# Two preactivation blocks in one kernel: the background work's big transfers counted double, and one operand load asked for earlier

## The chip, the cores and the metric

The kernel runs on one core of a Trainium2 chip. The metric is the device time in microseconds (us) of one execution. Five engines work side by side, each through its own instruction list in order: PE (TensorE, matrix products), DVE (VectorE), ACT (ScalarE), POOL (GpSimd) and SP (SyncE). Here SP does nothing but issue DMA transfers; every transfer of this kernel is issued from SP, so a transfer that has to wait for its data or its buffer holds back all that stand behind it in SP's list.

## The reference

The input `x` is 16 images of 64 x 64 pixels and 96 channels. Two blocks follow each other, each with a residual: `x = x + block(groupnorm(x))`.

```
# block 0: a two-layer channel MLP with a quadratic activation, on an image upsampled by
# two and band-limited (done here with small dense matrices); low-passed, every 2nd pixel kept
h = upsample(xn);  h = h @ W1.T + b1
h = coef0 + coef1 * h + coef2 * h * h
h = h @ W2.T + b2;  out = lowpass(h)[::2, ::2]

# block 1: a selective-scan block. d = 192 inner channels, 16 states, 4 scan directions
xz = x @ in_proj.T;  xc, z = split(xz);  z = silu(z)
xc = silu(depthwise_conv3x3(xc) + conv_b)
xs = [xc rows, xc columns, xc rows reversed, xc columns reversed]        # K = 4 directions, L = 4096
dts, Bs, Cs = split(x_proj @ xs);  delta = softplus(dt_proj @ dts + bias)
h_t = exp(delta_t * A) * h_(t-1) + (delta_t * u_t) * B_t                 # for every channel and state
y_t = sum over the states of h_t * C_t,  plus u_t * D
y = y0 + y2[::-1] + transposed(y1 + y3[::-1])
y = layernorm(y) * w + b;  out = out_proj @ (y * z)
```

The recurrence in `h_t` is the bulk of the work: 16 images x 4 directions x 192 channels x 16 states, each a chain of 4096 steps.

## The kernel before

**The foreground.** The function `scan` runs over 3072 *units*. A unit is one image, one quarter of the 4096 positions (`T` = 1024), one of six *blocks* (two groups, e = 1 and e = 0, of 32 channels in one direction) and one `j` (four of the 16 states). A block has four units, j = 0 to 3; a *step* (one pair of directions, one quarter) has six blocks, 24 units; an image has eight steps, 192 units. In the text "unit 101" is the unit counted from the start of its image.

In unit n the work on the engines is:

- POOL, `drive(n + 2)` (L794): b = dtu x B for both groups of the unit after next (128 x 2048).
- ACT, `decay(n + 1, e)` (L788), once for each group: da = exp(A x delta), into one PSUM tile for each group.
- DVE, `recur(n, e)` (L803 or L805), once for each group: the recurrence itself, a scan over 1024 positions.
- The product with C: for group 0 on DVE (L972), for group 1 on POOL (L963). In one unit of five (`SHARE`), called odd here, group 1's product is done on DVE as well (L954).
- PE, `read_out(n - 1)` (L827): sums over the states.

The order of a unit is written out by hand (the schedule is manual): group 1's scan, `decay(n + 1, 1)`, **slot 0**, POOL's product and `drive(n + 2)`, group 0's scan, `read_out(n - 1)`, **slot 1**, group 0's product, `decay(n + 1, 0)`, the store of a finished block, **slot 2**, and then loads for later units.

**The loads of the foreground.** For the block after the present one, `dtu` is asked for in the unit with j = 0, the tile `delta` of group 1 in the unit with j = 1, and the tile `delta` of group 0 in the unit with j = 2, behind slot 2. `delta` tiles have three buffers, so group 0's tile of the next block takes the place of group 1's tile of the present block. The last reader of that one is `decay(n + 1, 1)` of the unit with j = 2, which stands just ahead of slot 0. All these are issued at L715, 512 KB each. The B and C rows (`bt`, `ct`, L734) are asked for behind slot 2 too.

**The background.** Between the scans two other programs are advanced bit by bit: `front(mi + 1)`, which does block 0 and the convolution of the next image, and after it `finish(mi - 1)`, which does the layernorm and the output product of the image before. Both are Python generators: what lies between two `yield`s is a *slice*. A third generator, `project`, makes dtu, delta, B and C for the next step of 24 units. Each of the three slots of a unit calls `slot(position)`, which first takes a slice of `project` where one is due and then one of `front` or `finish`. A slice of these is due while `n * POS < at * SLICES`, where `at` counts the slots so far (`POS` = 576 an image), and `n` the slices taken: one for each, or the number that the generator yielded, so `HEAVY` counts as two. One slice at most is taken in a slot.

`front` begins with `parts(xt, xc[mi])`, the load of the next image in four transfers of 384 KB, one a slice. Then comes `norm` (two passes over the image on ACT, a few tiny operations, and at L237 `nb = nmean * rg` on DVE, 96 x 1), a small DVE addition `lin` (L260, 96 x 96), the four sweeps of block 0, the output of block 0 stored by `parts(made["x1"], x1)`, `norm` again, and twelve convolution tiles. After the matrix products of each tile the generator yields `WAIT`: the two Silu activations (L506, L507) need another ACT table set, so they run only in a slot 2 with no store pending (the gate). The unit after a gate is made odd, and while the gate is fresh `project` is held where it has yielded `BUSY`. At the end `parts(made["xs"][1], col)` stores 2 MB in four transfers. `finish` begins with two more `parts`, six loads of 512 KB (`ycol`, issued at L200 as all of `parts`).

Of the kernel before, what the change touches and what calls it, by code (L numbers as in the profile page):

```python
# [68 lines left out]
NEPS = 1e-5  # L69
BOTH = "natural_log_exp_and_others"  # L70
POS = 3 * 8 * 6 * NQ
SLICES = 499
WAIT = -1
BUSY = -2
HEAVY = 2
# [5 lines left out]
def tile_two_blocks(  # L81
# [114 lines left out]
    def parts(out, in_, n=4):  # L196

        step = L // n
        for i in range(n):
            nc.sync.dma_start(out=out[:, step * i:step * i + step], in_=in_[:, step * i:step * i + step])  # L200
            yield

    def norm(xt):

# [418 lines left out]
    def scan():  # L623


        with ExitStack() as es:
# [85 lines left out]
            def spread(out, what, ctx, bi, e):  # L712

                v, s0, r = blocks[bi]
                nc.sync.dma_start(  # L715
                    out=out,
                    in_=ctx[what][v][32 * (s0 + e):32 * (s0 + e) + 32, :].unsqueeze(1).to_broadcast([32, NQ, T]),
                )

            def fetch_dtu(ctx, bi):  # L720
                t = p2.tile([128, 2, T], F32, name="dtu")
                for e in range(2):
                    spread(t[:, e, :], "dtu", ctx, bi, e)
                return t

            def fetch_delta(ctx, bi, e):
                t = p3.tile([128, T], F32, name="delta")
                spread(t, "delta", ctx, bi, e)
                return t
# [11 lines left out]
            def fetch_y0(lc, bi):  # L741
                y0 = yp.tile([128, 2 * QT], F32, name="y0")
                nc.sync.dma_start(out=y0, in_=ypart[lc, bi])
                return y0
# [6 lines left out]
            bc, dtus, deltas = {}, {}, {}  # L751
# [33 lines left out]
            def decay(n, e):  # L785
                k, g = group(n, e)
                da = aps.tile([128, T], F32, name="da", tag=f"da{e}")
                nc.scalar.activation(da, deltas[n // NQ, e], AF.Exp, scale=a_s[:, k, g, units[n][2]:units[n][2] + 1])  # L788
                das[n, e] = da

            def drive(n):
                b = p4.tile([128, 2, T], F32, name="b")
                bt = bc[0, blocks[units[n][1]][2], units[n][2]]
                nc.gpsimd.tensor_mul(b, dtus[n // NQ], bt.unsqueeze(1).to_broadcast([128, 2, T]))  # L794
                bs[n] = b

            def recur(n, e, out):
                st, bi, j = units[n]
                pair = steps[st][1]
                da, b = das.pop((n, e)), bs[n][:, e, :]  # L800
                before = 0.0 if st % NT == 0 else states[bi][0][:, e, j:j + 1]
                if pair == 0:
                    nc.vector.tensor_tensor_scan(out, da, b, before, ALU.mult, ALU.add)  # L803
                else:
                    nc.vector.tensor_tensor_scan(out[:, ::-1], da[:, ::-1], b[:, ::-1], before, ALU.mult, ALU.add)  # L805

            def keep(n, e, h, copy):
                st, bi, j = units[n]
                if st % NT < NT - 1:
                    end = h[:, T - 1:T] if steps[st][1] == 0 else h[:, 0:1]  # L810
                    copy(states[bi][1][:, e, j:j + 1], end)  # L811
# [70 lines left out]
            def slot(position):  # L882
                nonlocal full, full_unit
                back = ahead_gen if ahead_gen.gen is not None else behind_gen
                back.at += 1
                step_gen.at += 1
                gate = back.said == WAIT and back.due() and position == 2 and storing is None
                if gate:
                    full, full_unit = 2, n + 1
                if step_gen.due() and not (full and step_gen.said == BUSY):  # L890
                    light = step_gen.said != BUSY
                    step_gen.step()

                    if light and step_gen.due() and step_gen.said != BUSY:
                        step_gen.step()
                if back.due() and (gate or back.said != WAIT):
                    back.step()
                full = max(full - 1, 0)

            last = len(units) - 1  # L900
            def next_step(st, mi):

                nonlocal step_gen
                if st < len(steps):
                    if steps[st][0] > mi:
                        ahead_gen.drain()
                    step_gen = Background(project(*steps[st], ctxs[st], gps), PSLICES, 3 * per_step)
# [8 lines left out]
            for n, (st, bi, j) in enumerate(units):  # L916
                mi, pair, lc = steps[st]
                v, s0, r = blocks[bi]
                m = n // NQ
                if n % per_image == 0:  # L920
                    image[mi]["y"] = dram.tile([2, DI, L], F32, name="y_d")
                    behind_gen.drain()
                    ahead_gen = behind_gen = nothing
                    if mi + 1 < B:
                        ahead_gen = Background(front(mi + 1), SLICES, POS)
                elif n % per_image == 2 and mi > 0:
                    behind_gen = Background(finish(mi - 1), SLICES, POS)
                if j == 0:
                    new = stp.tile([128, 2, NQ], F32, name="new", tag=f"st{bi}")
                    states[bi] = (states[bi][1] if states[bi] else None, new)  # L930

                if j == 0:
                    ahead = None
                    if bi + 1 < len(blocks):
                        ahead = ctxs[st], bi + 1
                    elif n + NQ <= last:
                        step_gen.drain()
                        ahead = ctxs[st + 1], 0
                        next_step(st + 2, mi)
                    if ahead:  # L940
                        dtus[m + 1] = fetch_dtu(*ahead)
                elif j == 1:
                    if ahead:
                        deltas[m + 1, 1] = fetch_delta(*ahead, 1)


                credit += 1
                odd_here = n == full_unit or credit >= SHARE
                if odd_here:
                    credit -= SHARE  # L950
                h = das[n, 1] if odd_here else bs[n][:, 1, :]
                recur(n, 1, h)
                if odd_here:
                    nc.vector.tensor_mul(bs[n][:, 1, :], h, bc[1, r, j])  # L954
                keep(n, 1, h, nc.scalar.copy if odd_here else nc.vector.tensor_copy)
                if n < last:
                    decay(n + 1, 1)
                slot(0)
                if storing is not None:
                    next(storing, 0)  # L960
                    storing = None
                if not odd_here:
                    nc.gpsimd.tensor_mul(h, h, bc[1, r, j])  # L963
                if n + 2 <= last:
                    drive(n + 2)

                h = das[n, 0]
                recur(n, 0, h)
                if n >= 1:
                    read_out(n - 1)  # L970
                slot(1)
                nc.vector.tensor_mul(bs[n][:, 0, :], h, bc[1, r, j])  # L972
                keep(n, 0, h, nc.scalar.copy)
                if n < last:
                    decay(n + 1, 0)
                if n >= 1 and units[n - 1][2] == NQ - 1:
                    storing = store(n - 1)
                    next(storing)
                slot(2)
                if j == 2 and ahead:  # L980
                    deltas[m + 1, 0] = fetch_delta(*ahead, 0)
                if j == NQ - 1 and n < last and steps[units[n + 1][0]][1] == 1:
                    st2, bi2, _ = units[n + 1]
                    y0s[steps[st2][2], bi2] = fetch_y0(steps[st2][2], bi2)


                at = n % per_step
                for what in range(2):
                    ahead_j = at - (2 * NQ - 1 + what)
                    if 0 <= ahead_j < NQ:  # L990
                        bc[what, 1, ahead_j] = fetch_bc(ctxs[st], 1, ahead_j, what)
                    ahead_j = at - (5 * NQ - 1 + what)
                    if 0 <= ahead_j < NQ and st + 1 < len(steps):
                        bc[what, 0, ahead_j] = fetch_bc(ctxs[st + 1], 0, ahead_j, what)
# [113 lines left out]
```

## Time and profile before

| what | value |
|---|---|
| time, median of 3 runs | 21079.41 us (21074.11 to 21098.74) |
| the profiled execution, own time | 21085.42 us |
| its span, first to last instruction | 21083.6 us |
| DVE busy | 19569.4 us, 93% of the span |
| POOL busy | 19498.8 us, 92% |
| PE busy | 16908.7 us, 80% |
| ACT busy | 13780.9 us, 65% |
| first scan starts, last scan ends | 494 us, 20917 us |

The profile counts an engine as busy from an instruction's start to its end, also where the instruction itself is held up inside. The first 494 us (the first image's `front`, before any scan) and the last 166 us (the last image's `finish`) lie outside the scans. DVE and POOL are nearly always busy in between; so the table alone doesn't tell which of them sets the time in which stretch. That is read from the waits of each, and from the order in time.

### The profile page before, as it was taken

What the parts mean: (1) busy time and instruction counts of PE and PEld (TensorE: products, weight loads), DVE (VectorE), ACT (ScalarE), POOL (GpSimd) and SP (SyncE); (2) the same over time, 40 slices, a digit from 0 to 9 for tenths busy, and PEclk for the clock granted to TensorE, in tenths of its full rate; (3) what the DMA queues carried; (4) which work ended last, traced back from release to release, by engine and by line L of the source; (5) the groups of instructions that cost most, each with busy time, mean ns of one, the idle gap of its engine ahead of it and who ended that gap; (6) DMA issues with size and microseconds to landing.
All of it is one profiled execution on the core that took longest, in us unless ns stands there. A gap on an engine that the chain in (4) does not pass through costs nothing. (4 is left out here: it accounts for less than half of the span.)

```text
span 21083.6 us, 273452 instructions
## 1 busy us (share of the span) xinstructions
PE 16908.7 (80%) x98988; PEld 7230.6 (34%) x98988; DVE 19569.4 (93%) x12983; ACT 13780.9 (65%) x20546; POOL 19498.8 (92%) x5538
## 2 busy tenths in 40 slices
PE   7876788888878788788788888888787787888856
PEld 4423324233343333324333242333433333243221
DVE  0999999999999999999999999999999999999997
ACT  4666666667666666666666666676666666666553
POOL 0999999999999999999999999999999999999996
PEclk8887888888889888898888988888898888988977
DMA  2565565655656566565665656556565665656654
GB/s 84 191 202 195 195 227 195 221 202 196 226 198 227 197 210 212 194 230 191 218 207 197 226 199 219 202 197 222 197 226 198 212 212 198 229 195 216 224 186 141
DMA packets 1855464, 4277.11 MB, mean 203 GB/s; under 512 B 449438, under 2 KB 548670, under 8 KB 1852062
## 3 DMA queue, kind: packets, MB, share of 16 engines
q1 hardware_dynamic: 1854110, 4259.62, 60.1%
q8 instruction: 781, 12.80, 0.3%
q14 instruction: 573, 4.69, 0.1%
HBM read 3380.58 MB, written 878.18 MB: 202 GB/s over the span
## 5 line engine op out<-in xcount | busy, mean ns | idle before, releaser
L794 POOL TENSOR_TENSOR b<-dtu,bt 128x2048 f32<-128x2048 f32 x3072 | 13895.8, 4532 | 581.2 <-DMA dtu<-dtu_d 465.1
L788 ACT ACTIVATE da<-delta,a_s 128x1024 f32<-128x1024 f32 x6144 | 6857.4, 1117 | 2562.1 <-DVE b L972 945.5
L963 POOL TENSOR_TENSOR b<-b,ct 128x1024 f32<-128x1024 f32 x2458 | 5797.1, 2358 | 836.9 <-DVE new L811 628.6
L827 PE MATMUL y<-b,fold_s 128*32 128x256 f32 x49152 | 3871.3, 437 | 1153.0 <-DVE b L972 680.8
L972 DVE TENSOR_TENSOR b<-da,ct 128x1024 f32<-128x1024 f32 x3072 | 3756.4, 1223 | 91.8
L803 DVE TENSOR_TENSOR_SCAN da<-da,new,b 128x1024 f32<-128x1024 f32 x1383 | 3245.3, 2347 | 72.7 <-ACT da L788 57.2
L805 DVE TENSOR_TENSOR_SCAN da<-da,new,b 128x1024 f32<-128x1024 f32 x1361 | 3193.0, 2346 | 99.7 <-ACT da L788 77.0
L827 PEld LDWEIGHTS y<-b,fold_s 128*32 128x32 f32 x49152 | 1388.5, 119 | 3876.9 <-issue 1464.0
L805 DVE TENSOR_TENSOR_SCAN b<-da,new,b 128x1024 f32<-128x1024 f32 x943 | 2208.7, 2342 | 139.3 <-ACT da L788 81.5
L803 DVE TENSOR_TENSOR_SCAN b<-da,new,b 128x1024 f32<-128x1024 f32 x921 | 2156.5, 2341 | 11.2 <-ACT da L788 10.5
L811 ACT COPY new<-da 128x1 f32<-128x1 f32 x2764 | 432.9, 157 | 2607.4 <-DVE b L972 2236.0
L488 PE MATMUL c_ps<-xgp,wtap_s 96*64 96x512 f32 (+1 forms) x4608 | 1728.2, 633 | 184.7 <-ACT row L506 179.4
L697 PE MATMUL s<-w,ident_s 128*128 128x512 f32 x1530 | 1167.2, 854 | 636.0 <-ACT w L692 614.2
L371 PE MATMUL h_ps<-xu,w1t_s 96*128 96x500 f32 x1920 | 1044.0, 643 | 299.9 <-ACT t L311 125.9
L383 PE MATMUL o_ps<-w2c_s,hsq 128*100 128x96 f32 x9600 | 1041.5, 266 | 178.1 <-ACT hsq L352 177.8
L677 PE MATMUL s<-pr,dtw_s 128*128 128x512 f32 x1530 | 928.5, 691 | 315.2 <-ACT delta L703 224.9
L805 DVE TENSOR_TENSOR_SCAN da<-da,b 128x1024 f32<-128x1024 f32 x482 | 1103.5, 2289 | 53.0 <-ACT da L788 43.1
L383 PEld LDWEIGHTS o_ps<-w2c_s,hsq 128*100 128x100 f32 x9600 | 975.0, 179 | 410.3 <-ACT hsq L352 232.1
L803 DVE TENSOR_TENSOR_SCAN da<-da,b 128x1024 f32<-128x1024 f32 x460 | 1053.0, 2289 | 36.8 <-ACT da L788 34.8
L697 PE MATMUL s<-e,ident_s 128*128 128x512 f32 x1530 | 1004.2, 745 | 0.0
L820 PE MATMUL y<-y,ident_s 128*128 128x512 f32 x768 | 524.2, 770 | 583.5 <-ACT yt L838 457.6
L488 PEld LDWEIGHTS c_ps<-xgp,wtap_s 96*64 96x64 f32 (+1 forms) x4608 | 583.1, 169 | 1121.7 <-issue 842.6
(143 smaller groups left out, 21936.5 us busy)
## 6 DMA issues: line engine op xcount, KB each, us to landing
dtu<-dtu_d SPq DMA_DIRECT2D x1536, 512.0 KB
delta<-delta_d SPq DMA_DIRECT2D x1536, 512.0 KB
bt<-rows SPq DMA_DIRECT2D x1024, 512.0 KB
ct<-rows SPq DMA_DIRECT2D x1024, 512.0 KB
u<-xs_d SPq DMA_DIRECT2D x893, 256.0 KB
dtu_d<-dtu SPq DMA_DIRECT2D x765, 256.0 KB
delta_d<-delta SPq DMA_DIRECT2D x765, 256.0 KB
xr<-in_x SPq DMA_DIRECT2D x768, 128.0 KB
```

What stands on the lines that cost most here:

```text
L371: nc.tensor.matmul(h_ps[j], lhsT=w1t_s[:, 128 * j:128 * (j + 1)], rhs=xu.rearrange("c p q -> c (p q)"), start=True, stop=True,)
L383: nc.tensor.matmul(o_ps[:, p, :], lhsT=hsq[j][:, UPS * p:UPS * (p + 1)], rhs=w2c_s[:, j, :], start=(j == 0), stop=(j == HB - 1),)
L488: nc.tensor.matmul(c_ps[p:p + n], lhsT=wtap_s[:, tap, 128 * i:128 * i + n], rhs=xgp[:, h0:h0 + 8, dx:dx + HW], start=(tap == 0), stop=(tap ...
L677: nc.tensor.matmul(s, lhsT=dtw_s[:, pair, v, :], rhs=pr, start=True, stop=True)
L697: nc.tensor.matmul(s, lhsT=ident_s, rhs=of, start=(k == 0), stop=(k == 3))
L788: nc.scalar.activation(da, deltas[n // NQ, e], AF.Exp, scale=a_s[:, k, g, units[n][2]:units[n][2] + 1])
L794: nc.gpsimd.tensor_mul(b, dtus[n // NQ], bt.unsqueeze(1).to_broadcast([128, 2, T]))
L803: nc.vector.tensor_tensor_scan(out, da, b, before, ALU.mult, ALU.add)
L805: nc.vector.tensor_tensor_scan(out[:, ::-1], da[:, ::-1], b[:, ::-1], before, ALU.mult, ALU.add)
L827: nc.tensor.matmul(y[32 * q:32 * q + 32, e, :], lhsT=fold_s, rhs=b[:, e, QT * q:QT * q + QT], start=(pair == 0 and j == 0 and e == 0), sto ...
L963: nc.gpsimd.tensor_mul(h, h, bc[1, r, j])
L972: nc.vector.tensor_mul(bs[n][:, 0, :], h, bc[1, r, j])
```

## The change

There are three edits. `parts` yields `HEAVY` in place of nothing, so that each of its slices counts as two. `SLICES` goes from 499 to 517: an image has 12 `parts` slices in `front` and 6 in `finish`, and 499 + 18 = 517, so that the background ends at the same place. The load of group 0's `delta` for the next block moves from behind slot 2 to directly behind slot 0 of the same unit.

```
-SLICES = 499
+SLICES = 517
...
         for i in range(n):
             nc.sync.dma_start(out=out[:, step * i:step * i + step], in_=in_[:, step * i:step * i + step])
-            yield
+            yield HEAVY
...
                 if n < last:
                     decay(n + 1, 1)
                 slot(0)
+                if j == 2 and ahead:
+                    deltas[m + 1, 0] = fetch_delta(*ahead, 0)
                 if storing is not None:
                     next(storing, 0)
                     storing = None
...
                 slot(2)
-                if j == 2 and ahead:
-                    deltas[m + 1, 0] = fetch_delta(*ahead, 0)
                 if j == NQ - 1 and n < last and steps[units[n + 1][0]][1] == 1:
```

No instruction is added or removed on any engine; what changes is where the background's instructions stand among the scans, and where one load of each block stands in SP's list.

More of the change, by code (lines that the diff above doesn't have):

```diff
@@ L71 @@
 POS = 3 * 8 * 6 * NQ
-SLICES = 499
+SLICES = 517
 WAIT = -1
@@ L200, in parts @@
             nc.sync.dma_start(out=out[:, step * i:step * i + step], in_=in_[:, step * i:step * i + step])
-            yield
+            yield HEAVY
     def norm(xt):
@@ L958, in scan @@
                 slot(0)
+                if j == 2 and ahead:
+                    deltas[m + 1, 0] = fetch_delta(*ahead, 0)
                 if storing is not None:
@@ L979, in scan @@
                 slot(2)
-                if j == 2 and ahead:
-                    deltas[m + 1, 0] = fetch_delta(*ahead, 0)
                 if j == NQ - 1 and n < last and steps[units[n + 1][0]][1] == 1:
```

## The prediction

> **What bounds the kernel now.** I read the page's busy shares first, then the waits of POOL and DVE, then the order in time at the places where POOL waits.
>
> ```profile
> PE 16908.7 (80%) x98988; PEld 7230.6 (34%) x98988; DVE 19569.4 (93%) x12983; ACT 13780.9 (65%) x20546; POOL 19498.8 (92%) x5538
> L794 POOL TENSOR_TENSOR b<-dtu,bt 128x2048 f32<-128x2048 f32 x3072 | 13895.8, 4532 | 581.2 <-DMA dtu<-dtu_d 465.1
> L963 POOL TENSOR_TENSOR b<-b,ct 128x1024 f32<-128x1024 f32 x2458 | 5797.1, 2358 | 836.9 <-DVE new L811 628.6
> ```
>
> POOL's two rows make up its whole busy time: 4.53 us in each unit and 2.36 in four of five, 6.42 us a unit. DVE needs two scans of 2.34, a product of 1.23, a second one in one unit of five, and some small things: 6.4 us too. The scans last from 494 to 20917 us, 6.65 us a unit. So POOL and DVE bound it together. POOL works 19494 us of these 20423 and idles 930, some 60 us an image in images 1 to 14, and to that idle time I reduce the change: a DVE stall under which POOL still has work costs nothing by itself.
>
> POOL's waits by releaser:
>
> ```profile
> POOL b L963 <- DVE new L811: 628.6, 296, 14.1
> POOL b L963 <- issue: 131.1, 53, 6.2
> POOL b L794 <- PE y L827: 87.6, 30, 3.8
> ```
>
> It waits for DVE's scans, hardly ever for a transfer. Summed by unit, the 60 us an image lie in three places: 7 after the first `norm` (units 6 to 9), 8 after the second (units 101 to 103), 30 around the convolution's gates (units 107 to 141). All else is 15, and units 142 to 155, where the background's last big transfers are, have 1.4.
>
> The second `norm`, image 5, DVE and then POOL:
>
> ```profile
> 7557.46 2.28 DVE L805 TENSOR_TENSOR_SCAN b<-da,b 128x1024 f32<-128x1024 f32 x1
> 7559.78 0.15 DVE L811 COPY new<-b 128x1 f32<-128x1 f32 x1
> 7560.16 8.14 DVE L237 TENSOR_TENSOR nb<-nmean,rg 96x1 f32<-96x1 f32 x1 [0.23 <-ACT rg L234]
> 7568.22 2.28 DVE L805 TENSOR_TENSOR_SCAN da<-da,b 128x1024 f32<-128x1024 f32 x1
> ```
>
> ```profile
> 7557.02 4.49 POOL L794 TENSOR_TENSOR b<-dtu,bt 128x2048 f32<-128x2048 f32 x1
> 7561.48 2.35 POOL L963 TENSOR_TENSOR b<-b,ct 128x1024 f32<-128x1024 f32 x1
> 7563.80 4.48 POOL L794 TENSOR_TENSOR b<-dtu,bt 128x2048 f32<-128x2048 f32 x1
> 7574.53 2.35 POOL L963 TENSOR_TENSOR b<-b,ct 128x1024 f32<-128x1024 f32 x1 [6.25 <-DVE new L811]
> ```
>
> A product of 96 x 1 takes 8.14 us: it ends at 7568.30, when POOL ends the last thing it can do. Outside the scans it takes 0.16. Then POOL has nothing until DVE has done two scans and a product: 6.25 us.
>
> The place that the load's move aims at, unit 143 of image 5, SP and then ACT:
>
> ```profile
> 7852.37 0.34 SPq L200 DMA_DIRECT2D ycol<-y_d  x1
> 7852.90 0.81 SPq L680 DMA_DIRECT2D rows<-pr  x2
> 7853.77 0.93 SPq L200 DMA_DIRECT2D ycol<-y_d  x2
> 7854.74 0.52 SPq L715 DMA_DIRECT2D delta<-delta_d  x1
> ```
>
> ```profile
> 7862.73 2.15 ACT L788 ACTIVATE da<-delta,a_s 128x1024 f32<-128x1024 f32 x2 [4.46 <-DMA delta<-delta_d]
> ```
>
> `delta` is issued behind three `ycol` and two `rows`, is 8 us under way, and ACT waits 4.46, DVE then 3.36. POOL works through from 7842.75 on.
>
> **What the skill says.** The Trainium skill, "SBUF — State Buffer", section "SBUF: two separate sides": a DVE operation with two SBUF inputs and a GpSimd operation exclude each other for the whole instruction. The trace agrees and adds that POOL's next instructions go first: the 30 `nb` inside the scans took 194.7 us, 6.5 each, and the 15 `lin` 37.8. "ScalarE: Activation LUTs", section "What ACT_TABLE_LOAD costs", gives 1283 ns for a load; the trace has 1.28 twice at each gate, so 2.56 us of ACT.
>
> **The change part by part.** I counted slices and slots through both programs, and the order of the DVE instructions in the changed one agrees. No instruction comes or goes.
>
> *Pace.* An image has 496 slices before by weight and 514 after, in 576 slots: the others come at 517/499 = 1.036 of the old rate, the 18 `parts` at half of it. The first `norm` comes 1.3 units later, the sweeps drift from 1 late to 2 early, the convolution is 0 to 2 early, `finish` starts 1 to 1.7 late and ends even.
>
> *The two locks and `lin`.* `nb` of the first `norm` moves from unit 6, slot 2 to unit 8, slot 0; that of the second from unit 101, slot 0 to unit 100, slot 1; `lin` from unit 7 to unit 8, both slot 2. At slot 0 POOL still has a product and a drive before it runs dry, and DVE then owes it two scans and a product. At slot 2 DVE owes one scan (2.5 us seen). At slot 1: a product and a scan, 1.2 + 2.3 + 0.2, about 4. Where the next unit is odd, POOL has a second drive to go and idles longer (10.4 seen at slot 2, 13.2 at slot 0, so about 11 at slot 1); that is one image in five.
> First `norm` after: (4 x 6.2 + 13.2)/5 = 7.6. `lin`, two slots behind `nb` now, finds POOL dry and falls to 0.2 us; before it met a drive and cost 3 us in four images of five. Before, `nb` and `lin` together: 6.8. So +0.8.
> Second `norm` after: (4 x 4 + 11)/5 = 5.4, and 0.6 that followed later and stays; before 8.2. So -2.2.
> Together -1.4 us an image, -21 us over 15. Ends: -52 (the first costs no more than before, the second as little as a lock at slot 2, 4.1 and 0.6) and +15 (`lin` locks as before, 2.4 an image more).
>
> *The delta load.* One DMA for each of 767 blocks, 512 KB, moved on SP ahead of what slots 1 and 2 issue: `project`'s stores (L680, L706, L707), its u loads, and the background's transfers; the B and C loads stood behind it and still do. It now waits for `decay(n + 1, 1)` right there. SP already waits for an ACT da at L715, 445 times, 2159.9 us: there it is ahead of the engines, and loads that stood in slots 1 and 2 now wait with it, 4.9 us on average. I cost that at nothing: stores there come from ACT or DVE work behind that decay, and loads are asked for several slots ahead. Without that cover PE's first product of a tile starts late by up to 4.9.
> The gain: ACT waits for `delta` 56 times, 123.9 us in all, 62 at unit 144 and 40 at unit 148. With `parts` spread, two of the `ycol` and no `rows` stand before the load at unit 142, so it goes some 3 us earlier into emptier queues; I expect the wait at 144 gone and that at 148 mostly. Under it POOL idles only 1.4 us an image in units 142 to 155: -1.3 x 15 = -20 us. Ends: 0, and -82 if DVE alone bounds it there (3.23 and 2.25 us of DVE stall, x 15).
>
> *The gates.* There are 12 gates before and after. Before, in units 106, 109, 111, 113, 122, 125, 127, 129, 131, 134, 137, 139; after, 105, 109, 111, 113, 121, 123, 125, 129, 131, 133, 135, 137. Where two gates lie two units apart, PE has a whole tile (ten products 0.86 us apart), `project`'s products and the sums of two units to do, and ACT waits:
>
> ```profile
> 7749.52 1.28 ACT L506 ACT_TABLE_LOAD   x1
> 7753.63 0.69 ACT L506 ACTIVATE row<-c_ps,convb_s 128x512 f32<-128x512 f32 x1 [2.83 <-PE c_ps L488]
> ```
>
> I priced each gate of after by the gate of before that has the same gap and the same place of `project`'s four identity products (L697). POOL idle before: 0.8, 0.9, 6.1, 3.0, 0, 1.8, 6.3, 3.3, 4.1, 1.3, 1.5, 1.7, sum 31. After: 0.8, 0.5, 6.1, 3.0, 0, 0.6, 2.4, 0.5, 4.1, 2.4, 6.1, 3.0, sum 29.5. So -1.4, -20 us; ends -75 and +90, 5 to 6 us an image.
>
> The sum is -21 - 20 - 20 = -61. The profiled execution took 21085, so 21024; the median of the runs is 6 lower, so 21018. I take 21020.
>
> **The rivals.**
> *DVE bounds more than I think.* The stalls at units 144 and 148 come back in full: -82 in place of -20, 20956. For it: DVE and POOL need the same 6.4 us a unit. Against it: POOL has no gap over 0.2 us from 7842.75 to past 7890.
> *Nothing comes of it.* The three terms are small differences of like things; the two locks trade places and the late load is hidden under POOL: 21079, within 40.
> *Slower: the gates crowd.* Eight of the gaps are two units after, six before; in before a gap of two costs 4.1 us of POOL idle on average, a gap of three 1.4. If the place of `project` decides less than I think, that is 2 x 2.7 = 5.4 us an image; with one unit more at POOL's rate (0.7) some +90 us, less the 41 of the other terms: 21130. It decides once two more short gaps cost over 1.4 us each. For it: five gates in a row, units 129 to 137, with no pause for ACT and PE to catch up. Against it: the last short gap of before, 137 to 139, cost 1.7.
> *The edits don't do what they say* is out: the slots are counted from the program.
>
> **How the numbers follow.** My sum 0.42, DVE 0.13, nothing 0.22, crowding 0.23. A measurement of this kernel tells about 0.2% (42 us) from no change. Of my sum's case 0.05 falls within 42 us: faster 0.52, same 0.25, slower 0.23. The range runs from between DVE's case and the lower ends together, 20935, to just short of crowding with the positive end of the locks, 21135. The likeliest case's own range is 20970 to 21070.
>
> **What would show it.** In the trace after: `nb` of the first `norm` longer (about 8 us on average, from 4.8), of the second shorter (about 5, from 8.1), `lin` at 0.2; the ACT wait for `delta` well below 123.9 us; POOL's idle time near 56 us an image, the convolution's part near 30. If the convolution's part is above 33 the gates crowd; if `delta`'s wait is gone and the time unmoved, POOL hid it.

## The result, and the profile after

The kernel after takes 21068.58 us (median of 12 runs, 21060.81 to 21082.98), the kernel before on the same chip 21084.57 (12 runs). The ratio is 0.9992, with a 95% interval from 0.9984 to 0.9999: 16 us, or 0.08%. The forecast was 21020, 60 us faster; by its number what came is the case "nothing comes of it", which had a chance of 0.22, though not for that case's reason, as the next lines show. The profiled execution has a span of 21066.6 us, 17 less than before.

Behind this small number lie larger ones that cancel. The trace after shows each step. First the two tiny DVE operations, each by its line (duration in ns: shortest, median, longest; first and last start):

```profile
L237 DVE TENSOR_TENSOR nb<-nmean,rg x32: 155/5984/13043, 38.5 to 19049.7; 96x1 f32<-96x1 f32 x32
```

```profile
L260 DVE TENSOR_TENSOR lin<-lin,ident_s x16: 239/244/246, 39.3 to 18459.0; 96x96 f32<-96x96 f32 x16
```

Split by their place, the `nb` of the first `norm` takes 8.7 us on average (4.8 before), that of the second 5.5 (8.1 before), and `lin` never meets POOL any more. These three are as forecast.

Then the load that the move aims at, in SP's order, image 5:

```profile
7846.24 0.34 SPq L200 DMA_DIRECT2D ycol<-y_d  x1
7846.68 0.52 SPq L715 DMA_DIRECT2D delta<-delta_d  x1
7847.29 1.00 SPq L680 DMA_DIRECT2D rows<-pr  x2
7848.35 0.41 SPq L200 DMA_DIRECT2D ycol<-y_d  x1
```

`delta` stands behind two `ycol` (the first, not shown, went 3.75 us earlier) and ahead of `rows`. What ACT waits for it in the whole run, before and after (us in all, times, longest):

```profile
ACT da L788 <- DMA delta<-delta_d: 123.9, 56, 5.3
```

```profile
ACT da L788 <- DMA delta<-delta_d: 16.3, 15, 2.8
```

POOL's waits in the kernel after, whose product with C is now L965:

```profile
POOL b L965 <- DVE new L811: 632.2, 256, 14.3
POOL b L965 <- issue: 161.1, 60, 6.3
POOL b L794 <- PE y L827: 45.6, 16, 3.8
```

The sums by releaser are nearly those of before. By place they are not. This is POOL's idle time in us an image, added up from the trace for images 1 to 14 of every kernel; "norm 1" is units 4 to 14, "norm 2" units 98 to 104, "gates" units 105 to 141. The times are medians; the idle times are those of the one profiled execution, which took up to 22 us more or less than the median:

| kernel | us, median | norm 1 | norm 2 | gates | 142-155 | other units | sum |
|---|---|---|---|---|---|---|---|
| before | 21084.6 | 8.3 | 8.3 | 31.3 | 1.4 | 11.1 | 60.4 |
| after | 21068.6 | 7.7 | 6.1 | 34.7 | 0.0 | 10.7 | 59.2 |
| delta_only | 21089.4 | 8.3 | 8.3 | 31.2 | 1.4 | 10.7 | 59.9 |
| pace_only | 21069.3 | 7.7 | 6.1 | 34.7 | 0.0 | 11.0 | 59.5 |
| heavy_finish | 21088.4 | 8.3 | 8.3 | 31.4 | 0.0 | 13.3 | 61.3 |
| old_gates_locks | 20997.1 | 7.7 | 6.0 | 31.1 | 0.0 | 9.0 | 53.8 |
| before_nolock | 20845.9 | 0.9 | 0.4 | 30.5 | 1.4 | 10.0 | 43.2 |
| after_nolock | 20848.7 | 0.0 | 0.7 | 34.9 | 0.0 | 8.1 | 43.7 |
| old_gates | 20795.2 | 0.1 | 0.7 | 31.5 | 0.0 | 9.6 | 41.9 |
| xt_8 | 20934.8 | 0.5 | 0.5 | 32.3 | 8.3 | 9.4 | 51.0 |
| xt_8_fwd | 20892.2 | 0.4 | 0.5 | 32.3 | 7.2 | 6.8 | 47.2 |

The gates took 3.4 us an image more, where the forecast had 1.4 less. One of them, the gate in unit 123 of image 5, on ACT:

```profile
7714.80 1.28 ACT L506 ACT_TABLE_LOAD   x1
7719.96 0.69 ACT L506 ACTIVATE row<-c_ps,convb_s 128x512 f32<-128x512 f32 x1 [3.88 <-PE c_ps L488]
```

ACT has loaded the table and waits 3.88 us for the last products of the tile, and no decay runs meanwhile. DVE's next scan waits 3.14 us for that decay, and POOL's next product of group 1 then waits for DVE:

```profile
7726.82 2.35 POOL L965 TENSOR_TENSOR b<-b,ct 128x1024 f32<-128x1024 f32 x1 [4.25 <-DVE new L811]
```

This gate was priced at 0.6.

### The profile page after: what moved, and what is told of

It is laid out like the page before. It is cut to its first block, busy times and chain, and to the rows that moved or that the text cites. A ratio compares the mean times of both kernels' runs of the same rounds, so it can differ in the third digit from the quotient of the medians.

```text
span 21066.6 us, 273374 instructions
## 1 busy us (share of the span) xinstructions
PE 16778.8 (80%) x98988; PEld 7138.4 (34%) x98988; DVE 19569.9 (93%) x12983; ACT 13799.6 (66%) x20546; POOL 19497.9 (93%) x5538
## 5 line engine op out<-in xcount | busy, mean ns | idle before, releaser
L965 POOL TENSOR_TENSOR b<-b,ct 128x1024 f32<-128x1024 f32 x2458 | 5809.6, 2364 | 861.9 <-DVE new L811 632.2
```

## The experiments

Three terms are to be told apart: the locks (the DVE operations that POOL shuts out), the delta load with the spread of the transfers, and the place of the gates.

**delta_only.** The load's move alone, the old pace (lines against the kernel before).

```
                 slot(0)
+                if j == 2 and ahead:
+                    deltas[m + 1, 0] = fetch_delta(*ahead, 0)
...
                 slot(2)
-                if j == 2 and ahead:
-                    deltas[m + 1, 0] = fetch_delta(*ahead, 0)
```

> The kernel before with the delta load alone moved ahead; the pace is the old one, so the locks (POOL idle 8.3 and 8.2 us an image) and the gates (31.2 us) should stay as they are. Three-term theory: ACT's wait for delta falls from 123.9 us to some 40 to 90, since the transfers of the ycol loads still crowd, POOL's idle time in units 142 to 155 falls from 1.4 to about 0.7 us an image, and the time by 5 to 15 us. Rival, DVE bounds there too: the 5.5 us an image of DVE stall come back for each part of the wait that goes, 30 to 60 us faster. Rival, the move holds up other loads on SP: slower by up to 20 us.

Measured: 21089.4, ratio 1.0002 (0.9994 to 1.001). ACT's wait falls to 70.1 us, that at unit 144 from 62 to 24, that at 148 stays at 40. POOL's idle time in units 142 to 155 doesn't move: 1.4. So the move by itself does what it says and brings nothing that can be measured (POOL's idle time was to fall to about 0.7, the time by 5 to 15 us); each of the rivals, 30 to 60 us faster and a cost on SP, is not seen either.

**pace_only.** The double count and the 517 alone (lines against the kernel after).

```
-                if j == 2 and ahead:
-                    deltas[m + 1, 0] = fetch_delta(*ahead, 0)
...
                 slot(2)
+                if j == 2 and ahead:
+                    deltas[m + 1, 0] = fetch_delta(*ahead, 0)
```

> The kernel after with the delta load back behind slot 2: only the counting of the parts and the 517 are left. Three-term theory: the locks stand where they do in the kernel after (POOL idle about 7.9 and 6.0 us an image) and so do the gates (about 34.6); ACT's wait for delta is small, under 50 us, since the transfers are spread; time within 15 us of the kernel after. Rival, the gain of the kernel after comes from the load's move alone and the pace only costs: then this one is slower than before by 20 us or more.

Measured: 21069.3, ratio 0.9994 (0.9986 to 1.0003), within a microsecond of the kernel after, with the same idle time at every place. ACT still waits 64.6 us for delta (under 50 was expected), 24 of it at unit 144, and POOL's idle time at units 142 to 155 is zero all the same. So whatever the kernel after has, good and bad, comes from the pace, as far as these runs can tell: the load's move adds nothing to it.

**after_nolock and before_nolock.** Both kernels with the two operations taken off DVE, in the same slots.

```
-        nc.vector.tensor_mul(nb, nmean, rg)
+        nc.scalar.activation(nb, nmean, AF.Identity, scale=rg)
...
-        nc.vector.tensor_add(lin, lin, ident_s[0:C, 0:C])
+        nc.gpsimd.tensor_add(lin, lin, ident_s[0:C, 0:C])
```

> The kernel after with nb computed on ACT (activation with scale rg) and the addition lin on POOL, in the same slots; so DVE has no operation with two SBUF inputs beside POOL. Three-term theory: POOL's idle time behind the two norms falls from 7.9 and 6.0 us an image to under 2 each, some 10 us x 15 = 150 us faster than the kernel after, about 20920; the gates stay at 34 to 35. Rival, DVE is late there because of the chain of ACT and PE ahead of nb and not because POOL shuts it out: then the stall moves to ACT and the time falls by less than 40 us.

> The kernel before with nb on ACT and lin on POOL, the same slots. Three-term theory: POOL idle behind the norms falls from 8.3 and 8.2 us an image to under 2 each, 13 x 15 = 190 us faster than before, about 20890, and so it is faster than the kernel after with the same edit by about 30 us (3.4 us an image of gates less 1.4 of delta, x 15). Rival, the gates' difference is noise and absorbed by POOL's backlog: the two kernels without locks are equal, or the one with the new pace is faster by the 20 us of the delta load.

Measured: 20848.7, ratio 0.9889 (0.9876 to 0.9903), and 20845.9, ratio 0.9891 (0.9876 to 0.9906). The locks cost the kernel after 220 us and the kernel before 239, more than expected, and POOL's idle time behind both norms is nearly gone. So the locks' shift is worth 239 - 220 = 19 us to the kernel after, for 21 forecast; but it is a small difference of large ones, and the four runs of before_nolock alone lie 41 us apart. Without locks the two kernels are equal (3 us apart, where 30 were expected): the gates cost the new pace 4.4 us an image more, and it gets as much back elsewhere. The trace shows where: in units 0 to 95 the time over 6.37 us a unit is 4.6 us an image with the old pace and 1.8 with the new one; units 142 to 155 idle 1.4 less. These two kernels differ in the load's move as well as in the pace, and none without locks was run with the pace alone. ACT's waits for a late `delta` in units 0 to 95, 26 us in the kernel before without locks, are all gone in the kernel after without locks; so the move may have a part in this gain.

**after_nb_ts.** The kernel after with the same product, still on DVE.

```
-        nc.vector.tensor_mul(nb, nmean, rg)
+        nc.vector.tensor_scalar(nb, nmean, rg, None, ALU.mult)
```

> The kernel after with nb as a tensor_scalar on DVE: nmean is its one tensor input, rg its scalar operand of one value a partition; same place, same slot. If the long nb comes from two SBUF tensor inputs against POOL's, the 30 nb inside the scans take some 0.15 to 0.2 us each in place of 7, POOL's idle time behind the norms falls from 7.7 and 6.1 us an image to under 2 and 2 (lin may meet POOL again and take up to 3 us), and the time is 100 to 200 us below the kernel after. If any small SBUF operation of DVE has to wait for POOL, or if nb waits for its data, it stays at 7 us and the time doesn't move.

Measured, one run: 20956.7, some 112 below the kernel after.

```profile
L237 DVE TENSOR_SCALAR nb<-nmean,rg x32: 197/200/209, 38.5 to 18950.0; 96x1 f32<-96x1 f32 x32
```

```profile
L260 DVE TENSOR_TENSOR lin<-lin,ident_s x16: 243/4402/9553, 39.3 to 18354.0; 96x96 f32<-96x96 f32 x16
```

0.2 us everywhere: same engine, slot and data, and no lock with one tensor input in SBUF. So it was not late data that held DVE. Nor was it the kind of instruction: `shift`, a TENSOR_TENSOR of the size of `nb` that stands just ahead of `lin` and has one of its inputs in PSUM, runs beside a busy POOL in 15 of its 16 places here and takes

```profile
L259 DVE TENSOR_TENSOR shift<-k_ps,cb_s x16: 145/145/155, 39.2 to 18353.9; 96x1 f32<-96x1 f32 x16
```

What is left is the second tensor input in SBUF. And `lin`, which keeps two, takes over: POOL isn't dry any more when it comes, and it takes 4.4 us (median) in place of 0.24. POOL's idle time behind the first `norm` falls only to 4.1 us an image for that reason (under 2 was expected), behind the second to 0.8. This is the link between the two that the forecast used, seen from the other side.

**heavy_finish.** The kernel before with the double count in the six `ycol` loads alone (`parts` yields what it is given here); gates and locks stay where they are.

```
-        yield from parts(ycol[0], y_d[1, 0:128, :])
-        yield from parts(ycol[1], y_d[1, 128:DI, :], 2)
+        yield from parts(ycol[0], y_d[1, 0:128, :], 4, HEAVY)
+        yield from parts(ycol[1], y_d[1, 128:DI, :], 2, HEAVY)
...
-                    behind_gen = Background(finish(mi - 1), SLICES, POS)
+                    behind_gen = Background(finish(mi - 1), SLICES + 6, POS)
```

> The kernel before with the double count in the six ycol loads of finish alone, and 505 for finish alone, so that locks and gates stand exactly where they stand before; the delta load stays behind slot 2. Three-term theory, now with the pace as the cause: POOL's idle time in units 142 to 155 falls from 1.4 us an image to near 0, ACT's wait for delta from 124 to under 70 us, and the time by some 20 us; locks 8.3 and 8.3, gates 31.3 unchanged. Rival, that 1.4 hangs on where the gates before it leave POOL's backlog: it stays, and the time is that of before.

Measured: 21088.4, ratio 0.9999 (0.9991 to 1.0008). POOL's stall is gone (ACT's wait for delta is 90.8 us, where under 70 was expected), and the time is no shorter. Two stretches of image 6 show how, units 142 to 155 and 156 to 191 (from:to and length in us; then busy us and instructions of PE, PEld, DVE, ACT, POOL; clock, DMA share, GB/s), the kernel before and then this one:

```profile
9131.61:9227.66 96.05, 77.70 (x351) 26.36 (x348) 88.03 (x67) 56.45 (x85) 93.61 (x28) 0.91 0.88 287
9227.66:9463.80 236.14, 211.74 (x918) 68.29 (x918) 230.64 (x152) 141.28 (x191) 232.82 (x68) 0.95 0.66 219
```

```profile
9139.56:9231.61 92.05, 75.22 (x340) 25.81 (x336) 86.96 (x64) 55.09 (x82) 92.05 (x28) 0.89 0.86 290
9231.61:9472.96 241.35, 214.26 (x929) 69.27 (x928) 232.29 (x153) 141.87 (x194) 235.04 (x68) 0.96 0.65 217
```

The first stretch is 4.0 us shorter and POOL is busy for all of it; the next is 5.2 longer. The gain of units 142 to 155 is given back by the end of the image. In the first stretch POOL has no slack at all, in the second it idles 6.3 us where it idled 3.3 (on average over images 1 to 14, 4.8 and 2.9). The kernel after, which has no stall in units 142 to 155 either, idles 2.8 in units 156 to 191, so there it is not given back. Whether the loss in heavy_finish is a backlog taken over or the new places of `finish`'s slices was not told apart.

**gap3_560 and nolock_560.** The kernel after without locks and with a faster background, with and without a least distance of three units between gates.

```
-SLICES = 517
+SLICES = 560
...
-                gate = back.said == WAIT and back.due() and position == 2 and storing is None
+                gate = back.said == WAIT and back.due() and position == 2 and storing is None and n >= gated + 3
                 if gate:
-                    full, full_unit = 2, n + 1
+                    full, full_unit, gated = 2, n + 1, n
```

> The kernel after without the two locks, in which a gate opens only three units or more behind the last one, and SLICES is 560 so that the background still ends in its image; counted from the program the gates are then in units 97, 101, 105, 109, 114, 117, 121, 125, 129, 133, 137, 141, no two of them two units apart. Crowding theory: a gate without a near neighbour costs POOL 1.4 us, so the gates' idle time falls from 34.9 to some 17 us an image and the time from 20849 to about 20580 (18 x 15). Rival, the forced odd units cost what they cost wherever they stand: idle time over 30, time within 40 us of 20849.

> The same without the rule, only SLICES 560: the gates are in units 97, 99, 101, 103, 113, 115, 117, 119, 121, 123, 125, 127, so ten of the eleven gaps are two units. Crowding theory: with 4.1 us for a gap of two the gates' idle time is some 43 us an image, 8 more than after, and the time about 20970; the opposite of the kernel with the rule, at the same pace of the background. Rival: within 40 us of 20849.

Measured: 20992.0, ratio 0.9954 (0.994 to 0.9967), and 21015.3, ratio 0.9966 (0.9953 to 0.9979). Both miss what was expected, the first by 410 us, and neither is within the 40 us of 20849 that the rival gave. The gates with no near neighbour idle POOL 31.4 us an image (units 98 to 141), those with ten short gaps 35.8, the kernel after without locks 35.6: 4.4 us between the extremes, or 0.4 for each short gap in place of the 2.7 that the rival of crowding had. (The gates of the two also stand in other units, so the 0.4 is not distance alone.) And the pace of 560 costs by itself: in units 0 to 95 the time over 6.37 us a unit is 10 us an image in both, after 1.8. So the distance of the gates is not what decides most, and a background that runs ahead isn't free.

**old_gates and old_gates_locks.** The kernel after, without and with its locks, with the gates held to the units of the kernel before (lines against the kernel after; the first has the edit of after_nolock too).

```
+GATES = (106, 109, 111, 113, 122, 125, 127, 129, 131, 134, 137, 139)
...
-                gate = back.said == WAIT and back.due() and position == 2 and storing is None
+                gate = back.said == WAIT and n % per_image in GATES and position == 2 and storing is None
```

> The kernel after without the two locks, with its gates held back to the twelve units in which the kernel before has them (106, 109, 111, 113, 122, 125, 127, 129, 131, 134, 137, 139); pace, sweeps and the delta load are those of the kernel after. Three-term theory: the gates' place alone makes POOL's idle time 34.9 in place of 30.5 us an image, so it falls back to about 31, units 0 to 95 keep the gain that the kernel after has there (excess over 6.37 us a unit 1.8 against 4.6 us an image), and the time goes from 20849 to about 20800. Rival, idle time that is taken away at one place comes back at the next, as at units 142 to 155 in the run with the double count in finish alone: the time stays within 20 us of 20849.

> The kernel after as it is, with its two locks, but with the gates held to the twelve units of the kernel before. Three-term theory: the locks are those of the kernel after (POOL idle 7.7 and 6.1 us an image), the gates those of the kernel before (31 in place of 34.7), so some 50 us faster than the kernel after, near 21018, the time that was forecast. Rival, with the locks the idle time only moves elsewhere: within 20 us of the kernel after.

Measured: 20795.2, ratio 0.9861 (0.9847 to 0.9874), 54 us below the kernel after without locks; and 20997.1, ratio 0.9955 (0.9943 to 0.9968), 72 below the kernel after. The idle time at the gates falls from 34.9 to 31.5 and from 34.7 to 31.1 us an image, as expected: 3.4 to 3.6 x 15 = 51 to 54 us. So at the gates themselves their place cost the kernel after a little over 50 us. Elsewhere the two runs do not agree. Without locks the units 0 to 95 were to keep their gain and did not: the time over 6.37 us a unit there rises from 1.8 to 3.4 us an image, the idle time in all falls by only 1.8 (27 us), and the profiled executions are 32 us apart where the medians are 54. With locks the other units idle less too, and the sum falls by 5.4 (81 us). So whether a part of the gates' gain comes back in the sweeps stays open. The first of the two is the fastest kernel of all, 1.4% and 1.3% below the two kernels; 1.1% of that is the locks.

**xt_8 and xt_8_fwd.** The kernel before without locks, with the image's four transfers counted double (`parts` yields what it is given) and `front` alone at 507; in the second also the load's move, the edit of delta_only.

```
-        yield from parts(xt, xc[mi])
+        yield from parts(xt, xc[mi], 4, HEAVY)
...
-                        ahead_gen = Background(front(mi + 1), SLICES, POS)
+                        ahead_gen = Background(front(mi + 1), SLICES + 8, POS)
```

> The kernel before without the two locks, in which the four slices of the image's load count double and front alone runs at 507: the sweeps come one unit late at first and end even, the first nine gates stand as before (then 133, 135, 138 for 134, 137, 139), the delta load and finish are as before. If the small gain that the kernel after shows in units 0 to 95 comes from where the sweeps' slices stand, the excess there falls from 4.6 us an image to 2 to 3 and the time by 20 to 40 us, from 20846 to about 20815; if it comes from the delta load alone, which here stays behind slot 2, the excess stays above 4 and so does the time, within 15 us.

> The kernel of the last run (locks gone, the image's load counted double, front at 507) with one more edit: the delta load directly behind slot 0. In that run delta came late at unit 144 by 11.6 us an image, and POOL idled 8.3 us an image in units 142 to 155. If the load was late because it stood behind the transfers of slots 1 and 2, ACT's wait falls from 277 us to under 100, that idle time to under 2 us an image, and the time by some 80 to 100 us, to about 20840. If it was late because the DMA engines are full there whatever its place in SP's list, both stay and the time with them.

Measured: 20934.8, ratio 0.9924 (0.9911 to 0.9938), 89 above its base where 30 less were hoped for. `front` ends earlier here, so all six `ycol`, one a slot, stand ahead of the `delta` of unit 142 (three in the kernel before). The question about units 0 to 95 is not decided: the time over 6.37 us a unit is 3.7 us an image there, between the 2 to 3 of the one answer and the over 4 of the other. ACT and POOL:

```profile
ACT da L788 <- DMA delta<-delta_d: 277.1, 65, 14.6
```

```profile
POOL b L963 <- DMA dtu<-dtu_d: 86.2, 10, 11.0
```

Now POOL does idle for the load: 8.3 us an image. The profile puts POOL's wait down to `dtu`; in order of time, in image 5, ACT waits 13.34 us for `delta`, DVE's scan 12.63 for ACT, and POOL then 8.63. With the move (xt_8_fwd): 20892.2, ratio 0.9906 (0.9891 to 0.9921), 43 us better than without it, half of what was expected, and 1.1 of the 8.3 us is all that goes in units 142 to 155. The larger part is in units 0 to 95, where the time over 6.37 us a unit falls from 3.7 to 1.7 us an image, some 30 us in all. ACT's waits at units 28 and 12 fall (58 to none, 30 to 17 us in all), that at unit 144 only from 176 to 110, and ACT still has

```profile
7784.94 2.15 ACT L788 ACTIVATE da<-delta,a_s 128x1024 f32<-128x1024 f32 x2 [8.44 <-DMA delta<-delta_d]
```

though SP issued the load at 7775.46: 9.5 us for 512 KB, behind four `ycol`, in a stretch (units 142 to 155 of image 5) where the DMA engines are busy for 0.83. There the place in the list helps little; where the transfers are spread, in pace_only, the same wait is 24 us with no move at all. The move is worth something where loads crowd. With the transfers spread, as in the kernel after, it has nothing left to gain: pace_only is as fast.

## Why the prediction was right or wrong

The measured time lies in the range and the sign is right, but the size is not: 16 us in place of 60. The range is 200 us wide and holds "no change" as well, so lying in it says little. By the table, x 15, the change of POOL's idle time is -42 us at the two norms, -21 in units 142 to 155, +51 at the gates and -6 elsewhere, -18 in all for -16 measured; the forecast had -21, -20, -20 and nothing. The gates' term is wrong by some 70 us, and it is in part luck that the norms' came larger and left the sum on the right side.

- **What bounds the kernel**: right. POOL's busy time is 19498 us in both, and the times of all kernels follow POOL's idle time x 15 to within some 30 us.
- **The locks**: right in the mechanism. Slot for slot the durations came as worked out (8.7, 5.5 and 0.24 us for 8, 5 and 0.2). Where the two operations of the first `norm` stand (units 6 to 12) POOL's idle time rises from 7.2 to about 7.7, +0.5 for +0.8; that behind the second falls by 2.2, as forecast. The rest of the fall at "norm 1" is in units 13 and 14 (0.9 to nothing), for which the forecast had no term. after_nb_ts shows the cause. The pair without locks gives -19 for -21, nearer than runs that lie 41 us apart can tell.
- **The delta load**: the wait at 144 is gone and POOL's idle time there fell from 1.4 to nothing, as forecast, but the cause was put in the wrong place: it goes with the pace and not with the load's move (pace_only 0.0, delta_only 1.4). And the step "-1.3 x 15 = -20 us" took idle time removed as time gained. heavy_finish removes the same 1.4 us and is no faster, since units 156 to 191 take it up; in the kernel after they do not. No run takes this term alone out of the kernel after.
- **The gates**: wrong, and this is the step that failed: "I priced each gate of after by the gate of before that has the same gap and the same place of `project`'s four identity products". Sum forecast 29.5 us an image, measured 34.7. Two gates stand out. That in unit 123 was priced at 0.6 and idled POOL 4.1; that in unit 125 was priced at 2.4 and took 4.0. The others differ too and nearly cancel: 131 took 5.3 for 4.1, 135 only 3.2 for 6.1. So gap and `project`'s place do not fix a gate's cost. The term was +51 us at the gates, against -20.
- **The rival "the gates crowd"**: its sum was right where mine was wrong (above 33, it said, and 34.7 came), its mechanism was not borne out: ten short gaps in place of none made 4.4 us (nolock_560, gap3_560). What counts is which unit each gate falls in; that was shown by putting the gates back, not by a rule for them. What `project`, the tile's products and the scans have pending in that unit may be the reason; no run tests it.
- **The rival "nothing comes of it"**: its number came and its reason did not. The terms are not small; they cancel.
- **The chances**: by the shares of the cases, faster should have had 0.50 and same 0.27, not 0.52 and 0.25.
- **What was not foreseen**: the sweeps of units 0 to 95 were moved too and had no term. Without locks they gain 2.8 us an image; with locks only some 0.7, the first `norm` included. Why is open. For the kernels with locks pace_only shows that the load's move has no part in it; without locks the move may: it alone took 2.0 us there between xt_8 and xt_8_fwd, as ACT's waits at units 12 and 28 fell.

## What to carry to other kernels

A pacing constant of background work moves every slice, and the large terms that it moves have both signs; where a change of pace brings 0.1%, look for the one place that lost and hold that one fixed (54 and 72 us here). Idle time that is removed counts only if the stretch behind it doesn't take it up: read two stretches, the one with the stall and the next. A tiny operation with two tensor inputs in SBUF that is long in the profile, and ends when a busy GpSimd ends, is one that GpSimd holds out; give it one such input, or another engine (here 1.1% with both operations on other engines, 0.5% in one run with one input for `nb` alone).

## What the runs showed of the hardware

In these runs a DVE operation with two SBUF tensor inputs that comes while POOL runs does not get its turn at the end of POOL's instruction. POOL's next ones go first as long as they are ready: up to 13.04 us for a product of 96 x 1 that takes 0.16 alone. In image 5 of the kernel after it waits through the end of one and three more:

```profile
6945.16 12.72 DVE L237 TENSOR_TENSOR nb<-nmean,rg 96x1 f32<-96x1 f32 x1
```

```profile
6942.13 4.54 POOL L794 TENSOR_TENSOR b<-dtu,bt 128x2048 f32<-128x2048 f32 x1
6946.62 2.35 POOL L965 TENSOR_TENSOR b<-b,ct 128x1024 f32<-128x1024 f32 x1
6948.92 8.95 POOL L794 TENSOR_TENSOR b<-dtu,bt 128x2048 f32<-128x2048 f32 x2
```

The same product with one input as a scalar for each partition takes 0.20 us beside the same POOL. I had not expected how far `lin` depends on it: with `nb` out of the way its median rose from 0.24 to 4.4 us, and a part of the gain was lost.
